# A graph attention layer on one core: the last stage in 25 units of 500 nodes, 20 of them between the closing steps of the edge loop

## The chip, the cores and the metric

The kernel runs on one core of a Trainium2 chip. The metric is the device time of one execution in microseconds (us). A core has a tensor engine (PE, with its weight loads shown apart as PEld), a vector engine (DVE), a scalar engine (ACT), GpSimd (POOL) and a queue engine (SP). SP and ACT issue ordinary DMAs, POOL issues DMAs with a list of row numbers (indirect ones), and all of them are carried by 16 DMA engines. Each engine works its instructions off in program order, so an instruction that waits holds up everything behind it on that engine.

## What is computed

The reference is a layer of graph attention over 12,500 nodes and 400,000 edges that are sorted by target node.

```python
h = relu(layernorm(x))
message = (h @ w_src + b_src)[src] + (h @ w_dst)[dst]
message = message * edge_weight * radial_mlp(edge_attr)      # 3 small layers
message = message @ w_sep + b_sep                            # 8 heads: 16 scores, 16 values each
score   = einsum(smooth_leaky_relu(message scores), alpha_dot)
att     = softmax of score over the edges of one target node
out     = x + segment_sum(value * att) @ w_proj + b_proj
```

The softmax's denominator is divided out last: each node has one row of 136 numbers, 128 sums of values and 8 sums of weights (one for each head), and the quotient goes through `w_proj` and is added to `x`.

## The kernel before, in words

A first stage works out the tables of `h @ w_src` and `h @ w_dst` and checks that the edges are sorted as the fast path needs. The number `bad` (L321) chooses between the fast path, `windows()`, and a slow one (L1450 to L1484). Only the fast one runs here.

`windows()` has 391 steps. A step takes 1,024 edges, which are two sections of 512 edges. A section's targets lie within a window of 64 nodes. In `step(k)` the instructions of several stages of different step numbers are written out one after the other: the gather of source rows on POOL (L862), the radial network, the message, the scores, and, 13 steps later (`LAG`), the sums of values and weights over each window. That last stage is step c = k - 13: `values` (L1060, L1062) multiplies the message by `w_v` and by the attention weight, `sums` (L1073, L1077) adds the edges up into a window of rows, `ob`, and SP stores it twice: whole into `win` (L1081) and, by two DMAs of 63 rows each to places that are read from a table, into `agg`, the table of node sums (L1085). A section's last node is often also the next one's first. Such nodes are put together apart from this: 13 blocks of 128 section ends are chained (L1117 to L1183), and the joined rows are scattered by POOL into `agg` after the windows (`scatter`, L1190 to L1197). The joined rows of the first eleven blocks are made during the main steps and kept in `obs_d`.

When the last main step is issued, the pool of loaded tiles is closed (`held.close()`), and 14 closing steps follow (j = 0 to 13, L1353 to L1363). They finish the 13 late steps and the last softmax group (its rows are moved by six small DMAs, `S<-Sp` at L980, and go through two scans, L1003 and L1008, an exponential and a transposition, L1030 and L1033). In each closing step from j = 2 on SP also loads the joined rows of one block (L1359), and POOL scatters them. Two buffers hold them. Blocks 11 and 12 are worked out in closing steps and behind them (L1340 to L1351 and L1366 to L1369).

All dependences between DMAs go by semaphores that the builder sets. Since the addresses of the `agg` stores are not known ahead, a store and a scatter wait for each other's landing, unless a line says that they need not. In the kernel before, that line is in `store` (L1086, only for sections from 768 on) and in `scatter`. Each DMA of SP and ACT counts up one of eight semaphores in turn, and is issued only when the previous DMA on the same semaphore has landed.

The last stage, `final` (L1386 to L1446), then loads `agg` by nine DMAs of 128 partitions with 12 rows each (L1396), and works on groups of 12 rows per partition: sums of weights plus 1e-16 (L1406), reciprocal (L1407), product (L1408), and for each four rows a transposition (L1419), a copy by ACT (L1422), the product with `w_proj` (L1430), the addition of `x` (L1433) and the store (L1434). `x` with its bias has been loaded by ACT's queue in closing steps j = 3 and later (L1382), as eight DMAs into one tile.

Of the kernel before, what the change touches and what calls it, by code (L numbers as in the profile page):

```python
# [21 lines left out]
F32 = mybir.dt.float32  # L22
BF16 = mybir.dt.bfloat16
I32 = mybir.dt.int32
# [8 lines left out]
H = 8  # L33
# [23 lines left out]
def gnn_kernel(ctx: ExitStack, tc: tile.TileContext, a: dict, out: bass.AP):  # L57
# [7 lines left out]
    NS = -(-E // SEC)  # L65
    NP = NS // 2
    NX = -(-NP // MP) * MP * PR
    assert NT * P == E and RC * RP == E and NT % TPI == 0 and NT % SORT_T == 0
    assert NB <= P and N < SKIP and E % T == 0 and NS % 34 == 0 and NP % 2 == 1

# [86 lines left out]
    with tc.tile_pool(name="node", bufs=2) as np_, tc.tile_pool(name="node1", bufs=1) as n1, \  # L157
# [19 lines left out]
        nc.vector.memset(cur[0:1, 0:1], -1)  # L177
        NH = NS // 17
        ends = n1.tile([NH, 17, 2], I32, name="ends")
        eb = n1.tile([P, NS, 2], I32, name="eb")  # L180
        wt = {name: const.tile(shape, F32, name="c_" + name) for name, shape in (
            ("b_src", [C, 1]), ("dot", [C, 1]), ("heads", [C, C]), ("fc_w1", [RAD, FC]), ("fc_b1", [FC, 1]),
# [4 lines left out]
        def load_targets():  # L187

            nc.sync.dma_start(out=cur[:, 1:CC + 1], in_=dst.rearrange("(p c) -> p c", p=P))
            at = dst[CC - 1:CC]  # L190
            with nc.allow_non_contiguous_dma(reason="single targets"):
                nc.sync.dma_start(out=cur[1:P, 0:1], in_=bass.AP(at.tensor, at.offset, [[CC, P - 1], [1, 1]]))
                at = dst[0:1]
                h = NH - 1
                nc.sync.dma_start(out=ends[0:h], in_=bass.AP(
                    at.tensor, at.offset, [[34 * SEC // 2, h], [SEC, 17], [SEC - 1, 2]]))
                at = dst[h * 17 * SEC:h * 17 * SEC + 1]
                nc.sync.dma_start(out=ends[h:NH, 0:16, :], in_=bass.AP(
                    at.tensor, at.offset, [[1, 1], [SEC, 16], [SEC - 1, 2]]))
                at = dst[(NS - 1) * SEC:(NS - 1) * SEC + 1]  # L200
                nc.sync.dma_start(out=ends[h:NH, 16, :], in_=bass.AP(
                    at.tensor, at.offset, [[1, 1], [E - 1 - (NS - 1) * SEC, 2]]))
# [103 lines left out]
        def fits():  # L306
# [11 lines left out]
            nc.tensor.matmul(tot[:, 0:1], cnt, ones[:, 0:1], start=False, stop=True, skip_group_check=True)  # L318
            sum_ = n1.tile([1, 1], F32, name="sum_")
            nc.vector.tensor_reduce(sum_, tot, AX.X, ALU.add)  # L320
            nc.vector.tensor_copy(bad, sum_)  # L321
            nc.sync.dma_start(out=ends_d[:, 1:2 * NS + 1].rearrange("o (p c) -> (o p) c", p=NH),
                              in_=ends.rearrange("p s i -> p (s i)"))
            none = n1.tile([1, 2], I32, name="none")
# [422 lines left out]
    def windows():  # L747
# [7 lines left out]
        with tc.tile_pool(name="ps", bufs=1, space=PSUM) as pp, \  # L755
# [327 lines left out]
            def store(c, f):  # L1083
                at = nc.sync.value_load(base[0:1, f, c:c + 1])
                st = nc.sync.dma_start(out=agg[ds(at, W - 1), :], in_=accs[c][f * W:(f + 1) * W - 1, :])  # L1085
                if 2 * c + 1 >= (NC - 1) * (P // 2):  # L1086
                    tc.declare_no_dep(st.ins, group="combined", reason="its rows follow those of the blocks")


            def load_x(i):  # L1090
# [99 lines left out]
            def scatter(g):  # L1190
# [4 lines left out]
                    bounds_check=N - 1, oob_is_err=False)  # L1195
                tc.declare_no_dep(st.ins, group="combined", reason="each node's row is written once")
                tc.add_to_no_dep_group("combined", st.ins)  # L1197

            comb = {}

            def combined(g):
                comb[g] = tail_pool.tile([P, ROW], F32, name="comb", bufs=2)
                return comb[g]

            stages = {0: lambda g: (block_load(g), block_rows(g)), 2: block_maxima, 4: block_factors,
                      5: block_columns, 6: block_totals, 8: block_out}
# [122 lines left out]
            held.close()  # L1329


            tail_pool = held.enter_context(tc.tile_pool(name="fin1", bufs=1, side="right"))
            x_fin = tail_pool.tile([P, NB, C], F32, name="x_fin")
            x_loads = load_xb(x_fin)
            last = NC - 1

            def out_rows(g):
                block_rows_out(g, combined(g))
                scatter(g)

            jobs = {
# [10 lines left out]
            assert SB * (NC - 1) + LAG + 1 == NP + 7  # L1352
            for k in range(NP, NP + LAG + 1):  # L1353
                step(k)
                j = k - NP
                if j in jobs:
                    jobs[j]()
                if 0 <= j - 2 < NC - 2:
                    nc.sync.dma_start(out=combined(j - 2), in_=obs_d[(j - 2) * P:(j - 1) * P, :])  # L1359
                    scatter(j - 2)  # L1360
                if j >= 3:
                    next(x_loads, None)
            for _ in x_loads:  # L1363
                pass
            block_rows(last)
            block_columns(last)  # L1366
            block_totals(last)
            out_rows(last)
            work.close()  # L1369
            with tc.tile_pool(name="fin", bufs=3) as fp:  # L1370
                final(fp, x_fin, lambda i: pp.tile([P, 4, P], F32, name=("pm0", "pm1", "V")[i % 3]),
                      lambda i: pp.tile([P, 4, C], F32, name=("p3", "pa", "m1")[i % 3]))


    XQ = 12
    out_v = out[0:NF * P, :].rearrange("(p t) c -> p t c", t=NF)
    agg_v = agg[0:NF * P, :].rearrange("(p t) c -> p t c", t=NF)

    def load_xb(x_fin):

        for t0, t1 in groups:
            nc.scalar.dma_start(out=x_fin[:, t0:t1, :], in_=xb_v[:, t0:t1, :])  # L1382
            yield
        nc.scalar.dma_start(out=x_fin[:tail, NF, :], in_=xb[NF * P:N, :])
        yield

    def final(fp, x_fin, turned, product):
        starts = list(range(0, NB, XQ))
        gs, qs, qTs = {}, {}, {}

        def load_g(i):

            gs[i] = fp.tile([P, XQ, ROW], F32, name="g", bufs=len(starts))
            for n, t0, t1 in blocks(starts[i], min(starts[i] + XQ, NB)):
                o = starts[i]
                nc.sync.dma_start(out=gs[i][:n, t0 - o:t1 - o, :],  # L1396
                                  in_=agg_v[:, t0:t1, :] if n == P else agg[NF * P:N, :].unsqueeze(1))

        def quotients(i):
            r = fp.tile([P, XQ, H], F32, name="r")  # L1400
            qs[i] = fp.tile([P, XQ, C], F32, name="q")
            g = gs.pop(i)
            for n, t0, t1 in blocks(starts[i], min(starts[i] + XQ, NB)):
                s = slice(t0 - starts[i], t1 - starts[i])
                m = t1 - t0
                nc.vector.tensor_scalar(r[:n, s, :], g[:n, s, C:ROW], 1e-16, None, op0=ALU.add)  # L1406
                nc.vector.reciprocal(r[:n, s, :], r[:n, s, :])  # L1407
                nc.vector.tensor_mul(  # L1408
                    qs[i][:n, s, :].rearrange("p t (h k) -> p (t h) k", h=H),
                    g[:n, s, 0:C].rearrange("p t (h k) -> p t h k", h=H),  # L1410
                    r[:n, s, :].unsqueeze(3).to_broadcast([n, m, H, C // H]))

        def turn(i):
            t0, t1 = quads[i]
            q, o = qs[t0 // XQ], t0 // XQ * XQ
            pt = turned(i)
            for t in range(t0, t1):
                n = rows(t)
                nc.tensor.transpose(pt[:, t - t0, :n], q[:n, t - o, :], ident[:n, :n])  # L1419
            w = (t1 - t0 - 1) * P + rows(t1 - 1)  # L1420
            qTs[i] = fp.tile([P, 4, P], F32, name="qT")
            nc.scalar.copy(qTs[i].rearrange("p u n -> p (u n)")[:, :w], pt.rearrange("p u n -> p (u n)")[:, :w])  # L1422

        def finish(i):
            t0, t1 = quads[i]
            qT = qTs.pop(i)
            py = product(i)
            for t in range(t0, t1):
                n = rows(t)
                nc.tensor.matmul(py[:n, t - t0, :], qT[:, t - t0, :n], w_proj, start=True, stop=True)  # L1430
            for n, u0, u1 in blocks(t0, t1):
                y = x_fin[:n, u0:u1, :]
                nc.vector.tensor_add(y, py[:n, u0 - t0:u1 - t0, :], y)  # L1433
                nc.sync.dma_start(out=out_v[:, u0:u1, :] if n == P else out[NF * P:N, :].unsqueeze(1), in_=y)  # L1434

        for i in range(len(starts)):
            load_g(i)
        quotients(0)
        turn(0)
        for i in range(Q):  # L1440
            if i % 3 == 1 and i // 3 + 1 < len(starts):
                quotients(i // 3 + 1)
            if i + 1 < Q:
                turn(i + 1)
            finish(i)


    unfit = nc.values_load(bad[0:1, 0:1], min_val=0, max_val=2 * E)
    with tc.If(unfit == 0) as fit:
        windows()  # L1450
    with fit.Else():
# [7 lines left out]
        with tc.tile_pool(name="bias", bufs=1) as op:  # L1459
# [15 lines left out]
        with tc.tile_pool(name="fin_b", bufs=3) as fp, tc.tile_pool(name="fin1_b", bufs=1) as f1, \  # L1475
                tc.tile_pool(name="fin_ps", bufs=2, space=PSUM) as fps, tc.manual_schedule():
            x_fin = f1.tile([P, NB, C], F32, name="x_fin")
            for _ in load_xb(x_fin):
                pass
            final(fp, x_fin, lambda i: fps.tile([P, 4, P], F32, name="pt"),  # L1480
                  lambda i: fps.tile([P, 4, C], F32, name="py"))


# [34 lines left out]
```

## Time and profile before

| | |
|---|---|
| median of three executions | 4234.25 us (4232.47 to 4238.16) |
| profiled execution | 4228.57 us, of which 4226.8 us are the span of the profile |
| busy in the span | PE 93%, DVE 74%, POOL 71%, ACT 45% |
| last main step's message leaves PE | about 4057 us |
| closing steps | about 4058 to 4144 us |
| last scatter issued, first load of `agg` issued | 4153.97, 4156.12 us |
| last addition | 4219.58 us |

How to read it: the profile gives for a line of the kernel the engine, the operation, the tile written and the tiles read, how often it ran, and what ended the idle time before it. The view by windows gives for a stretch of time how long each engine was busy, the granted clock of PE (1.00 is full), the mean busy share of the 16 DMA engines and the GB/s that they moved. The trace also holds each DMA packet with its size, start and duration. A packet is one contiguous run of bytes. The times in the views count from the start of the span.

### The profile page before, as it was taken

To read this page: it belongs to the slowest core of one execution; us is meant where nothing else is said; L and a number is where in the kernel's file an instruction comes from. 1 tells how busy PE (TensorE), PEld (TensorE's weight loads), DVE (VectorE), ACT (ScalarE), POOL (GpSimd) and SP (SyncE) were. 2 spreads that over 40 slices of the span, in tenths; PEclk is the share of its full clock that TensorE was granted. 3 is DMA by queue.
4 is the path that set the end of the run, shared out by engine and by line. 5 is a ranking of instruction groups with operands and counts; after the bars stand their busy time and mean duration, and the time that the engine had idled before them with its cause. 6 is when DMAs were issued, how large, how long until landed. Compare 5 with 4: busy or idle time off the path is not lost. (4 is left out here: it accounts for less than half of the span.)

```text
span 4226.8 us, 87991 instructions
## 1 busy us (share of the span) xinstructions
PE 3921.2 (93%) x29351; PEld 2394.1 (57%) x29351; DVE 3124.1 (74%) x6334; ACT 1919.2 (45%) x4597; POOL 2987.1 (71%) x3147
## 2 busy tenths in 40 slices
PE   6779999999999999999999999999999999999975
PEld 5345555555555555555555555555555555555554
DVE  6567777777777777777777777777777777777754
ACT  6344444444444444444444444444444444444421
POOL 0777777777777777777777777777777777777710
PEclk9889999999999999999999999999999999999988
DMA  6766776676776776676676676666766766666634
GB/s 217 218 193 178 189 195 178 195 194 185 189 198 188 187 194 187 182 195 189 186 193 194 183 192 179 179 184 185 187 183 180 189 180 183 188 178 185 184 86 160
DMA packets 593333, 783.08 MB, mean 185 GB/s; under 512 B 125553, under 2 KB 392302, under 8 KB 592740
## 3 DMA queue, kind: packets, MB, share of 16 engines
q1 hardware_dynamic: 384786, 514.16, 40.0%
q0 software_dynamic: 100416, 205.44, 22.2%
q10 hardware_dynamic: 107666, 57.76, 4.6%
q8 instruction: 234, 3.83, 0.4%
q14 instruction: 231, 1.89, 0.2%
HBM read 637.83 MB, written 139.30 MB: 184 GB/s over the span
## 5 line engine op out<-in xcount | busy, mean ns | idle before, releaser
L862 POOL DMA_INDIRECT gs<-t_src,idx x3125 | 2972.9, 951 | 1055.6 <-issue 802.6
L951 ACT ACTIVATE sl<-pa,c_b_a 128x512 f32<-128x512 f32 x782 | 536.9, 687 | 1021.1 <-PE pa L949 1006.6
L956 DVE SCALAR_TENSOR_TENSOR al<-pa,sl 128x512 f32<-128x512 f32 x782 | 540.4, 691 | 594.2 <-ACT sl L951 571.3
L1060 PEld LDWEIGHTS V<-c_w_v,mT 128*128 128x128 f32 x6048 | 746.6, 194 | 292.2 <-DVE ob L1077 122.3
L1060 PE MATMUL V<-c_w_v,mT 128*128 128x128 f32 x6048 | 879.1, 289 | 0.0
L949 PE MATMUL pa<-mT,c_w_a 128*128 128x512 f32 x1564 | 814.6, 603 | 3.5 <-DVE mT L943 2.6
L1062 DVE TENSOR_TENSOR pvx<-V,Pem 128x512 f32<-128x512 f32 x756 | 519.0, 687 | 243.7 <-PE V L1060 231.9
L929 PEld LDWEIGHTS pm<-ident,gs 128*128 128x128 f32 x3125 | 393.6, 142 | 421.3 <-issue 338.4
L1073 PEld LDWEIGHTS misc<-pvx,oh 128*64 128x64 f32 x6250 | 353.8, 138 | 408.4 <-ACT h L885 395.2
L921 DVE SCALAR_TENSOR_TENSOR rad<-p,c_fc_b,w_b 128x512 f32<-128x512 f32 x782 | 550.2, 745 | 39.5 <-PE p L913 4.3
L1073 PE MATMUL misc<-pvx,oh 128*64 128x136 f32 x6250 | 455.6, 288 | 116.1 <-ACT h L885 108.5
L943 DVE SCALAR_TENSOR_TENSOR mT<-pm,c_b_src,rad 128x512 f32<-128x512 f32 x782 | 550.7, 746 | 3.1 <-PE pm L936 3.1
L899 ACT ACTIVATE h<-p,b 128x512 f32<-128x512 f32 x391 | 287.5, 735 | 420.0 <-PE p L896 380.9
L929 PE MATMUL pm<-ident,gs 128*128 128x128 f32 x3125 | 472.3, 274 | 0.2 <-DMA gs<-t_src,idx 0.2
L913 PE MATMUL p<-h,w3b 64*128 64x512 f32 x1564 | 405.8, 596 | 12.5 <-ACT h L899 12.5
L936 PE MATMUL pm<-ohT,m 64*128 64x512 bf16 x2346 | 322.4, 381 | 0.0
L982 ACT ACTIVATE Sp<-m,b_s 128x512 f32<-128x512 f32 x192 | 131.9, 687 | 394.2 <-PE m L965 394.2
L881 PE MATMUL m<-eT,w1b 64*128 64x256 f32 x782 | 274.5, 431 | 27.6 <-DVE M L1003 18.1
L881 PE MATMUL misc<-eT,w1b 64*128 64x256 f32 x782 | 274.4, 431 | 0.0
L1046 DVE TENSOR_TENSOR oh<-lane,misc 128x504 f32<-128x504 f32 x391 | 262.2, 671 | 0.1
L896 PE MATMUL p<-h,w2b 64*64 64x256 f32 x3128 | 259.8, 402 | 0.6 <-DVE rad L921 0.6
L949 PEld LDWEIGHTS pa<-mT,c_w_a 128*128 128x128 f32 x1564 | 241.7, 195 | 20.7 <-DVE mT L943 6.2
(172 smaller groups left out, 3680.4 us busy)
## 6 DMA issues: line engine op xcount, KB each, us to landing
w_b<-in_edge_weight SPq DMA_DIRECT2D x390, 512.0 KB
d_b<-in_dst SPq DMA_DIRECT2D x390, 256.0 KB
gs<-t_src,idx POOLq DMA_INDIRECT x3125
e_t<-in_edge_attr ACTq DMA_DIRECT2D x390, 128.0 KB
sc_d<-Sp SPq DMA_DIRECT2D x192, 256.0 KB
win<-ob SPq DMA_DIRECT2D x391, 68.0 KB
agg<-ob SPq DMA_DIRECT2D x782, 33.5 KB
md<-t_dst SPq DMA_DIRECT2D x782, 32.0 KB
```

The source lines that it names most:

```text
L862: nc.gpsimd.indirect_dma_start(out=gs[:, t, :], out_offset=None, in_=t_src[:, :], in_offset=bass.IndirectOffsetOnAxis(ap=idx[:, t0 + t:t0 ...
L881: nc.tensor.matmul(p1[q], w1b[s, :], eTs[k][s, :], start=True, stop=True)
L913: nc.tensor.matmul(p3s[k][:, f, 0:SEC], w3b[s, :], h2s[k][s, :], start=True, stop=True)
L921: nc.vector.scalar_tensor_tensor(rad[:, s], p3[:, f, 0:n], b3, w_g[k][:, s], op0=ALU.add, op1=ALU.mult)
L929: nc.tensor.matmul(pms[k, f][:, t * T:(t + 1) * T], gs[:, t, :], ident, start=(t == 0), stop=False, is_transpose=True, skip_group_check=True)
L943: nc.vector.scalar_tensor_tensor(mTs[k][:, s], pms.pop((k, f))[:, 0:n], b_n, rad[:, s], op0=ALU.add, op1=ALU.mult)
L949: nc.tensor.matmul(pa[:, 0:n], w_a, mTs[k][:, f * SEC:f * SEC + n], start=True, stop=True)
L951: nc.scalar.activation(sl[:, 0:n], pa[:, 0:n], AF.Silu, bias=b_a, scale=1.0)
L956: nc.vector.scalar_tensor_tensor(al, pa, 0.25, sl, op0=ALU.mult, op1=ALU.add)
L1060: nc.tensor.matmul(V[:, t, :], mTs[c][:, o:o + T], w_v, start=True, stop=True)
L1062: nc.vector.tensor_mul(pvx[c][:, f, 0:n, 0:C].rearrange("p t (h k) -> p t h k", h=H), V[:, 0:n, :].rearrange("p t (h k) -> p t h k", h=H), ...
L1073: nc.tensor.matmul(acc[f * W:(f + 1) * W, :], ohs[c][:, f * TS + t, :], pvx[c][:, f, t, :], start=(t == 0), stop=(t == n - 1), skip_group_ ...
```

## The change

Nothing changes in the 391 main steps. Behind them:

- The last stage works in 25 units of 500 nodes, as 125 partitions with 4 rows each. A unit has one load of 125 x 2,176 bytes from `agg`, one of 125 x 2,048 bytes of `x`, and one store of 125 x 2,048 bytes.
- Units 0 to 19 are worked off within the closing steps: two per step for j = 4 to 11, one for j = 12 and 13, and two beside the last block. Units 20 to 24 follow the last scatter. Loads of early units and all loads of `x` are issued by ACT, loads of `agg` for the last five by SP.
- The first seven loads of `x` are issued ahead of closing step 0, the first seven loads of `agg` in closing step 3; later ones follow unit by unit.
- The joined rows of eleven blocks are loaded by one DMA (`ready`) ahead of closing step 0 and scattered by eleven instructions in a row.
- Stores of sections from 704 on do not wait for these eleven scatters. They are no longer exempt from waiting for the scatter of block 11.
- The check of the fast path also asks that section 704 begins at node 10,000 or later. In the given input it begins at node 10,146, so the fast path is taken.

```diff
             def store(c, f):
...
-                if 2 * c + 1 >= (NC - 1) * (P // 2):
-                    tc.declare_no_dep(st.ins, group="combined", reason="its rows follow those of the blocks")
+                if 2 * c >= EARLY_S:
+                    tc.declare_no_dep(st.ins, group="early", reason="its rows follow those of the early blocks")
+                    tc.add_to_no_dep_group("later", st.ins)
...
-            x_loads = load_xb(x_fin)
+            fin = held.enter_context(tc.tile_pool(name="fin", bufs=2, side="right"))
             last = NC - 1
+            ready = fin.tile([P, last - 1, ROW], F32, name="ready", bufs=1)
+            nc.sync.dma_start(out=ready, in_=obs_d[0:(last - 1) * P, :].rearrange("(g p) c -> p g c", p=P))
+            for g in range(last - 1):
+                comb[g] = ready[:, g, :]
+                scatter(g)
+            un = Units(fin, 8, 9, lambda u: pp.tile([P, 4, P], F32, name=("V", "pa")[u % 2]),
+                       lambda u: pp.tile([P, 4, C], F32, name=("p3", "m1")[u % 2]))
+            un.load_x(0, 7)
...
             for k in range(NP, NP + LAG + 1):
                 step(k)
                 j = k - NP
                 if j in jobs:
                     jobs[j]()
-                if 0 <= j - 2 < NC - 2:
-                    nc.sync.dma_start(out=combined(j - 2), in_=obs_d[(j - 2) * P:(j - 1) * P, :])
-                    scatter(j - 2)
-                if j >= 3:
-                    next(x_loads, None)
-            for _ in x_loads:
-                pass
+                if j == 3:
+                    for u in range(7):
+                        un.load_g(u)
+                    un.quotients(0)
+                    un.quotients(1)
+                    un.turn(0)
+                if j >= 4:
+                    un.run(2 if j < 12 else 1, EARLY)
             block_rows(last)
+            un.run(1, EARLY)
             block_columns(last)
+            un.run(1, EARLY)
             block_totals(last)
             out_rows(last)
...
-            with tc.tile_pool(name="fin", bufs=3) as fp:
...
+            un.open(EARLY, NU)
+            un.run(NU, NU)
+            un.close(NU)
...
+    UP, UT = 125, 4
...
+        def view(self, t, u):
+            return t[u * UN:(u + 1) * UN, :].rearrange("(p t) c -> p t c", t=UT)
...
+        def load_x(self, u0, u1):
+            for u in range(u0, u1):
+                if u < NU and u not in self.x:
+                    self.x[u] = self.pool.tile([UP, UT, C], F32, name="xu", bufs=self.nx)
+                    nc.scalar.dma_start(out=self.x[u], in_=self.view(xb, u))
...
+        def load_g(self, u):
+            self.g[u] = self.pool.tile([UP, UT, ROW], F32, name="g", bufs=self.ng)
+            eng = nc.scalar if u < EARLY else nc.sync
+            ld = eng.dma_start(out=self.g[u], in_=self.view(agg, u))
...
+        def finish(self, u):
+            qT, py, y = self.qT.pop(u), self.product(u), self.x.pop(u)
+            for t in range(UT):
+                nc.tensor.matmul(py[:UP, t, :], qT[:, t, :], w_proj, start=True, stop=True)
+            nc.vector.tensor_add(y, py[:UP], y)
+            nc.sync.dma_start(out=self.view(out, u), in_=y)
+            self.nf = u + 1
...
+        def run(self, n, end):
+            for _ in range(n):
+                u = self.nf
+                v = max(self.g, default=u) + 1
+                if v < end:
+                    self.load_g(v)
+                while self.nq < min(u + 3, end):
+                    self.quotients(self.nq)
+                while self.nt < min(u + 2, end):
+                    self.turn(self.nt)
+                self.finish(u)
+                self.load_x(u + 7, u + 8)
```

`quotients` is the addition, the reciprocal and the product of a unit on DVE (now written in place), `turn` four transpositions and ACT's copy, `finish` four products, the addition and the store.

More of the change, by code (lines that the diff above doesn't have):

```diff
@@ L67, in gnn_kernel @@
     NX = -(-NP // MP) * MP * PR
+    NU = 25
+    EARLY = 20
+    EARLY_S = (-(-2 * NS // P) - 2) * (P // 2)
     assert NT * P == E and RC * RP == E and NT % TPI == 0 and NT % SORT_T == 0
@@ L179, in gnn_kernel @@
         ends = n1.tile([NH, 17, 2], I32, name="ends")
+        lim = n1.tile([1, 1], I32, name="lim")
         eb = n1.tile([P, NS, 2], I32, name="eb")
@@ L192, in load_targets @@
                 nc.sync.dma_start(out=cur[1:P, 0:1], in_=bass.AP(at.tensor, at.offset, [[CC, P - 1], [1, 1]]))
+                at = dst[EARLY_S * SEC:EARLY_S * SEC + 1]
+                nc.sync.dma_start(out=lim, in_=at.unsqueeze(1))
                 at = dst[0:1]
@@ L320, in fits @@
             nc.vector.tensor_reduce(sum_, tot, AX.X, ALU.add)
-            nc.vector.tensor_copy(bad, sum_)
+            low = n1.tile([1, 1], F32, name="low")
+            nc.vector.tensor_scalar(low, lim, float(EARLY * (N // NU)), None, op0=ALU.is_lt)
+            nc.vector.tensor_add(bad, low, sum_)
             nc.sync.dma_start(out=ends_d[:, 1:2 * NS + 1].rearrange("o (p c) -> (o p) c", p=NH),
@@ L1197, in scatter @@
                 tc.add_to_no_dep_group("combined", st.ins)
+                if g < NC - 2:
+                    tc.declare_no_dep(st.ins, group="later", reason="its rows precede those of the later sections")
+                    tc.add_to_no_dep_group("early", st.ins)
+                else:
+                    tc.declare_no_dep(st.ins, group="early", reason="its rows follow those of the early units")
+                    tc.add_to_no_dep_group("later", st.ins)
             comb = {}
-            def combined(g):
-                comb[g] = tail_pool.tile([P, ROW], F32, name="comb", bufs=2)
-                return comb[g]
             stages = {0: lambda g: (block_load(g), block_rows(g)), 2: block_maxima, 4: block_factors,
@@ L1329, in windows @@
             held.close()
-            tail_pool = held.enter_context(tc.tile_pool(name="fin1", bufs=1, side="right"))
-            x_fin = tail_pool.tile([P, NB, C], F32, name="x_fin")
-            x_loads = load_xb(x_fin)
+            fin = held.enter_context(tc.tile_pool(name="fin", bufs=2, side="right"))
             last = NC - 1
+            ready = fin.tile([P, last - 1, ROW], F32, name="ready", bufs=1)
[6 more added lines that the diff above has]
+            un.load_x(0, 7)
             def out_rows(g):
-                block_rows_out(g, combined(g))
+                comb[g] = fin.tile([P, ROW], F32, name="comb")
+                block_rows_out(g, comb[g])
                 scatter(g)
@@ L1351, in windows @@
             }
-            assert SB * (NC - 1) + LAG + 1 == NP + 7
+            assert SB * (NC - 1) + LAG + 1 == NP + 7 and EARLY == 20
             for k in range(NP, NP + LAG + 1):
@@ L1365, in windows @@
+                if j >= 4:
+                    un.run(2 if j < 12 else 1, EARLY)
             block_rows(last)
+            un.run(1, EARLY)
             block_columns(last)
+            un.run(1, EARLY)
             block_totals(last)
             out_rows(last)
+            un.run(NU, EARLY)
+            un.close(EARLY)
             work.close()
-            with tc.tile_pool(name="fin", bufs=3) as fp:
-                final(fp, x_fin, lambda i: pp.tile([P, 4, P], F32, name=("pm0", "pm1", "V")[i % 3]),
-                      lambda i: pp.tile([P, 4, C], F32, name=("p3", "pa", "m1")[i % 3]))
@@ L1375, in gnn_kernel @@
[L1375 to L1445, printed above, removed]
@@ new lines, in windows, with __init__, quotients, turn @@
+            un.open(EARLY, NU)
+            un.run(NU, NU)
+            un.close(NU)
+    UP, UT = 125, 4
+    UN = UP * UT
+    assert N % UN == 0 and NU == N // UN
+    class Units:
+        def __init__(self, pool, nx, ng, turned, product):
+            self.pool, self.nx, self.ng, self.turned, self.product = pool, nx, ng, turned, product
+            self.x, self.g, self.qT = {}, {}, {}
+            self.nq = self.nt = self.nf = 0
+        def view(self, t, u):
[9 more added lines that the diff above has]
+            ld = eng.dma_start(out=self.g[u], in_=self.view(agg, u))
+            if u < EARLY:
+                tc.declare_no_dep(ld.ins, group="later", reason="their nodes follow those of the early units")
+                tc.add_to_no_dep_group("early", ld.ins)
+        def quotients(self, u):
+            g = self.g[u]
+            r = self.pool.tile([UP, UT, H], F32, name="r")
+            nc.vector.tensor_scalar(r, g[:, :, C:ROW], 1e-16, None, op0=ALU.add)
+            nc.vector.reciprocal(r, r)
+            q = g[:, :, 0:C].rearrange("p t (h k) -> p t h k", h=H)
+            nc.vector.tensor_mul(q, q, r.unsqueeze(3).to_broadcast([UP, UT, H, C // H]))
+            self.nq = u + 1
+        def turn(self, u):
+            g, pt = self.g.pop(u), self.turned(u)
+            for t in range(UT):
+                nc.tensor.transpose(pt[:, t, :UP], g[:, t, 0:C], ident[:UP, :UP])
+            self.qT[u] = self.pool.tile([P, UT, UP], F32, name="qT")
+            nc.scalar.copy(self.qT[u], pt[:, :, :UP])
+            self.nt = u + 1
+        def finish(self, u):
+            qT, py, y = self.qT.pop(u), self.product(u), self.x.pop(u)
+            for t in range(UT):
+                nc.tensor.matmul(py[:UP, t, :], qT[:, t, :], w_proj, start=True, stop=True)
+            nc.vector.tensor_add(y, py[:UP], y)
+            nc.sync.dma_start(out=self.view(out, u), in_=y)
+            self.nf = u + 1
+        def open(self, u0, u1):
+            for u in range(u0, u1):
+                self.load_g(u)
+            self.load_x(u0, u1)
+        def run(self, n, end):
+            for _ in range(n):
+                if self.nf >= end:
+                    return
+                u = self.nf
[8 more added lines that the diff above has]
+                self.load_x(u + 7, u + 8)
+        def close(self, end):
+            while self.nf < end:
+                self.run(1, end)
@@ L1474, in gnn_kernel @@
               ea_s.rearrange("(t p) c -> p t c", p=P), "b")
[L1475 to L1481, printed above, removed]
+        with tc.tile_pool(name="fin_b", bufs=3) as fp, tc.tile_pool(name="fin_ps", bufs=2, space=PSUM) as fps, \
+                tc.manual_schedule():
+            un = Units(fp, 10, 10, lambda u: fps.tile([P, 4, P], F32, name="pt"),
+                       lambda u: fps.tile([P, 4, C], F32, name="py"))
+            un.load_x(0, 7)
+            for u in range(7):
+                un.load_g(u)
+            un.run(NU, NU)
 def kernel(**inputs):
```

## Prediction

> **What bounds the kernel now.** I read the chain that ended last, then the waits and the timeline of the stretch behind the main steps, then the windows. The chain lies wholly in the last stage:
>
> ```profile
> DVE q L1408 0%; PE pm L1419 0%; PE m L1430 0%; PE p L1430 0%; DVE r L1407 0%; DVE x_fin L1433 0%; DVE r L1406 0%; DVEq L1406 0%
> ```
>
> Ahead of it stand the closing steps. The waits from 4040 to 4160 us, of SP's queue and of the engines, say what slows them:
>
> ```profile
> SPq L1085 <- DMA agg<-comb,ids: 20.6, 4, 11.4
> ...
> POOL agg L1192 <- DMA comb<-obs_d: 49.7, 10, 11.1
> ```
>
> Each store of windows waits for the scatter before it, each scatter for its load, and the load stands in SP's queue behind the store. So the closing steps last from 4058 to 4144 us, though PE is busy for only 5.5 of the 21 us from 4092 to 4113. Then the hand-over, in the timeline:
>
> ```profile
> 4153.97 0.90 POOL L1192 DMA_INDIRECT agg<-comb,ids  x1 [4.36 <-POOLq L1449]
> 4156.12 6.59 SPq L1396 DMA_DIRECT2D g<-agg  x10
> 4160.77 0.21 DVE L1406 TENSOR_SCALAR r<-g 128x96 f32<-128x96 f32 x1 [7.92 <-issue]
> 4161.02 0.75 DVE L1407 RECIPROCAL r<-r 128x96 f32<-128x96 f32 x1
> 4161.80 1.76 DVE L1408 TENSOR_TENSOR q<-g,r 128x1536 f32<-128x1536 f32 x1
> ```
>
> From the first load to the span's end are 4226.8 - 4156.1 = 70.7 us. They are what the change wants to hide.
>
> **What the DMAs can carry** decides this change, since every new load and store has 125 rows. Before has DMAs of 125 rows too: the clearing of `agg`, `agg<-z` (L139), packets of 2,720 bytes. The windows of its last burst and of the loads of `agg`:
>
> ```profile
> 228.00:240.00 12.00, 0.00 (x0) 0.00 (x0) 0.00 (x0) 0.00 (x0) 8.98 (x10) 0.51 0.45 155
> 4157.00:4171.00 14.00, 5.10 (x28) 4.70 (x29) 6.18 (x8) 1.76 (x3) 0.00 (x0) 0.64 1.00 403
> ```
>
> In the first row PE, DVE and ACT stand still and the DMA engines are busy for 0.45 only. In the second, loads of 128 rows fill all 16 (4158 to 4172: 420 GB/s, 26.2 per engine). The timeline shows the price of the first:
>
> ```profile
> 225.09 3.30 SPq L139 DMA_DIRECT2D agg<-z  x2
> ...
> 229.76 0.36 SPq L983 DMA_DIRECT2D sc_d<-Sp  x1
> ...
> 238.95 0.58 SPq L988 DMA_DIRECT2D S<-sc_d  x1
> ...
> 242.63 1.22 DVE L1003 TENSOR_TENSOR_SCAN M<-m,S 128x512 f32<-128x512 f32 x1 [17.79 <-DMA S<-sc_d]
> ```
>
> A 256 KB store behind two such DMAs took 8.8 us to land. The packet records say why. Of the 2,720-byte packets at most 7 or 8 are in flight at once, with two DMAs outstanding or four; of the 2,048-byte packets of 128 rows 17 to 21. The z bursts move 73 to 81 GB/s. If the 125 rows run on n engines, each of these carries 1/n of z and 1/16 of the rest. In the seven bursts n = 5 gives 21.7 to 27.9 GB/s per engine (first burst: 136 KB + 105 KB in 8.64 us), the saturated rate; n = 8 gives 22.0 in the first burst and less in the others. So I take five, always the same five, 25 packets on each: 5 x 26.2 = 131 GB/s.
>
> The Trainium skill, "DMA: Bandwidth & Descriptors", section "Why a DMA increments its semaphore by 16 and not by 1", says that a DMA issued by SP or ACT uses the largest number of engines up to 16 that divides its row count: five for 125. The trace agrees in a second case: the 63-row stores of windows end in nine small increments, those of 128 rows in sixteen. The same page's section "Anatomy of one DMA — SWDGE (gpsimd) path" fits 2.0 us plus bytes at 436 GB/s, under which nothing here would be bound by DMA; that is the first rival.
>
> **The change part by part.** A unit needs 125 x 2,176 bytes (272 KB, 2.08 us at 131 GB/s) and twice 256 KB (1.95 us each): 5.98 us of the five engines.
>
> *Its compute* costs less. DVE: addition 0.17 (between 0.16 for 8 columns and 0.20 for 96), reciprocal 0.35 (0.20 and 0.75), product 0.69 (0.29 for 128 columns, 1.76 for 1,536), addition of x 0.69: 1.90 us. PE: 0.60 + 1.06 = 1.66 us (L1419, L1430). A closing step without stalls takes PE 2.05 + 1.15 = 3.2 us (L1060, L1073), DVE 2.5 us. Two units in it: PE 6.5, DVE 6.3 us, and some 7.0 with their waits for each other. The DMAs of two units take 12 us. So from closing step 4 on, the five engines set the pace, not PE or DVE.
>
> *Ahead of closing step 0:* seven loads of x, 7 x 1.95 = 13.7 us of the five engines, from 4058.6 (the last main product on DVE, L943, whose tiles' room they take) to about 4075 with 2 us to land. Semaphores are taken in turn by eight DMAs, so a DMA waits for the landing of a stranger; before shows it as
>
> ```profile
> SPq L139 <- DMA e_t<-in_edge_attr: 7.7, 3, 3.7
> ```
>
> In the changed order the six `S<-Sp` (L980, at 4065 to 4069 before) come eight places behind the fifth to seventh load of x. They are then issued until 4078 or so, and the scan at 4070.46 (L1003), the exponential and the copy that ends at 4081.7 (L1033) move by 9 us (0 if no wait falls there, 13 if the loads also hold up ACT's work). ACT waits in its own queue as well: the seventh load for `ready`, and behind it stand the last `Silu` and the scores, some 6 us, within these 9.
>
> *The eleven scatters* need 11 x 1.25 us (the gather's 0.94 + 0.30), from about 4068 to 4082, and 2.2 us to land (4105.12 to the store at 4107.33). The first load of `agg`, now at 4081.7 + 9 = 4091, hides them. If each took the 6.75 us from the first scatter to the next store (4086.34 to 4093.09), they would end at 4144 and add 50 us; nothing but x loads in flight explains that one, so I leave it out.
>
> *What goes:* the waits of stores for scatters, 20.6 us, and eleven loads with their turns. That time is filled by the units. The new wait of a store for the scatter of block 11 holds only later stores, under 5 us, beside the same DMAs.
>
> *From 4091 on* the five engines carry 25 loads of agg, 18 of x and 25 stores: 52.0 + 35.1 + 48.8 = 135.9 us. ACT issues a load of x only when a unit's store has landed (eight buffers), but with five or so large DMAs outstanding the engines do not run dry. The windows' own stores cost each of the five 69.6 KB / 16 + 2 x 34.3 KB / 9 = 12 KB a step, 0.46 us, 13 times 6 us. First byte 1.0 us (4156.12 to the first packet of `agg` at 4157.11). The last block's chain (sums 4142.35 to load 4156.12 before, 13.8 us) runs beside the late stores and loads of x, which last about as long; I set 3 us for what is not covered. From the last data to the end 3 us (the last large packets end at 4222.2, the span at 4226.8, with two small stores between).
>
> **Sum:** 4091 + 1 + 135.9 + 6 + 3 + 3 = 4240 us of span against 4226.8: 13 us slower, 4242 against the profiled execution's 4228.57. That lies 5.7 us under the median shown, so on the median's scale 4234.25 + 13.2 = **4247.5 us**.
>
> Both ends: at the z bursts' 79 GB/s the 17.8 MB would take 225 us, 90 us more. But there the engines also carried the rest. At 131 with the delay ahead at nothing and the small stores hidden, it is 4240 - 9 - 6 = 4225.
>
> **The rivals.**
> *A, not slower: the rows spread over more engines.* With 16, a unit is 1.9 us of DMA and compute sets the pace. The loads land early, closing step 4 begins near 4090, eight steps of 7.0 us and two short ones end the last sums near 4153, the last loads go out 12 us later at 4165, and with 3.2 us to land, 12.5 for five units (five times 1.9 and the way in) and 6.7 to the end the span is 4187: -39 us, 4195. The change wins from six engines on, since 142 us then become 118. The 7 or 8 packets in flight (against 17 to 21 for sixteen, by ratio some 6 engines) leave this open; that 125 does not divide by 6, 7 or 8 speaks against it.
> *B, no change: five engines, but no delay ahead and full overlap:* 4225 of span, 4233.
> *C, slower still: the queues wait for one another.* A load of x waits for a store, the store in SP's queue for a window, ACT holds copies behind its load, and the five engines run dry for 1.5 us per early unit: 30 us more, 4277. The 8.8 us of the store at 229.76 speak for it.
> That the change does nothing is not possible here: section 704 begins above node 10,000.
>
> **How the numbers follow.** Forecast 0.55, A 0.15, B 0.15, C 0.15. Within 0.2% (8.5 us, about what a measurement of this kernel tells from no change) lie most of B and a little of the forecast: 0.18. Faster: A and a little of B, 0.18. Slower: 0.64. The range reaches from below B, 4222, over the forecast to most of C, 4285; A is left out.
>
> **What would show it.** Right: after 4091 the DMA share stays near 0.3 to 0.4 with 130 to 170 GB/s while PE and DVE wait on loads of g or x; L1003 of the last group near 4079; at most 8 packets of 2,048 or 2,176 bytes in flight; closing steps of 10 us and more. Wrong: loads of units at 300 GB/s, PE over 90% in the closing steps, the last scatter before 4170.

## The result, and the profile after

The changed kernel takes 4273.41 us (median of four runs, 4271.84 to 4279.97), the kernel before beside it 4233.36 us (four runs, 4232.17 to 4238.16): a ratio of 1.0095, 95% interval 1.0081 to 1.0108. It is slower by 40 us. The forecast was 4247.5 us, 13 us slower, within 4222 to 4285.

The profiled execution took 4274.37 us, its span 4272.6 us. The profile page of the changed kernel, the chain that ended last:

```profile
DMA g<-agg 0%; DMA agg<-comb,ids 0%; PE p L1446 0%; PE m L1446 0%; PE pa L1438 0%; PE V L1438 0%; DVE g L1432 0%; DVE xu L1447 0%; DVE r L1430 0%; SPq L1421 0%; DVE r L1429 0%; POOLq L1476 0%
```

It now begins with transfers: the load of a unit's sums, and ahead of it the last scatter. Before, it held only DVE and PE. The windows of the closing steps, the hand-over and the last units (us, then busy time and instructions of PE, PEld, DVE, ACT and POOL, granted clock, DMA share, GB/s):

```profile
4113.00:4144.00 31.00, 17.01 (x140) 15.29 (x138) 16.94 (x41) 3.56 (x9) 0.00 (x0) 0.82 0.36 134
4144.00:4171.00 27.00, 16.35 (x99) 14.85 (x100) 9.52 (x23) 2.75 (x10) 0.00 (x0) 0.69 0.36 131
4171.00:4210.00 39.00, 26.48 (x196) 24.03 (x195) 21.74 (x50) 5.53 (x15) 0.97 (x1) 0.85 0.35 129
...
4230.00:4250.00 20.00, 3.16 (x13) 2.40 (x13) 1.32 (x5) 0.56 (x2) 0.90 (x1) 0.50 0.22 72
4250.00:4273.00 23.00, 10.40 (x60) 9.65 (x60) 9.31 (x20) 2.88 (x5) 0.00 (x0) 0.65 0.30 104
```

In none of them is PE or DVE busy for 70% of the time, and in none do the 16 DMA engines reach a share of 0.4. That is the sign the prediction named: five engines full, eleven nearly empty. The packet records say it outright. From the first load of `agg` at 4101.46 us to the end, at most 8 packets of 2,048 or 2,176 bytes are in flight; while any is, the mean is 4.9; and for only 11.3 of the 171.1 us none is. Each DMA of a unit also ends in small increments, packets of 4 bytes: five behind each of the five late loads of `agg` (the first at 4249.09 to 4249.48 us). In the experiments below there are 14 behind a late store of 126 rows, 16 behind one of 128 and one behind one of 127. So the number five does not hang on packets in flight alone.

What waits is in SP's queue (total us, times, longest):

```profile
SPq L1093 <- DMA agg<-ob: 55.4, 18, 6.5
...
SPq L1093 <- DMA xu<-xb: 11.8, 5, 5.7
...
SPq L1093 <- DMA agg<-comb,ids: 5.7, 1, 5.7
```

The waits of stores for scatters went from 20.6 to 5.7 us, as predicted. The stores of windows now wait for their own forerunners: 55.4 us from 4062 us on, against 12.2 in the closing steps of the kernel before (4040 to 4160 us). With units of 128 rows (e1 below) it is 16.0, so it is the narrow transfers that hold these stores up.

The timeline at the start of the closing steps (start, duration, engine, line, operation, tiles):

```profile
4062.90 12.23 ACTq L1416 DMA_DIRECT2D xu<-xb  x7
...
4075.17 0.34 ACT L1048 COPY pvx<-Pem 128x32 f32<-128x32 f32 x2 [12.47 <-DMA win<-ob]
...
4084.17 4.90 SPq L988 DMA_DIRECT2D S<-Sp  x6
...
4090.65 1.22 DVE L1011 TENSOR_TENSOR_SCAN M<-m,S 128x512 f32<-128x512 f32 x1 [5.24 <-DMA S<-Sp]
```

ACT stands in its queue for 12.2 us until the seventh load of `x` is issued. The last scores come behind it and end at 4080.4, their six small transfers start at 4084, behind stores of windows in SP's queue, and the scan at 4090.65 (before: 4070.46; the prediction named 4079). The closing steps with two units take 11.5 to 15.4 us each, as it said. And the hand-over to the last five units:

```profile
4229.99 0.84 SPq L1140 DMA_DIRECT2D rr<-win  x2
...
4236.72 0.28 PE L1172 MATMUL misc<-ident,rr 28*128 28x28 f32 x1 [10.71 <-DMA rr<-win]
...
4241.47 0.90 POOL L1201 DMA_INDIRECT agg<-comb,ids  x1 [36.03 <-POOLq L1476]
4245.17 2.71 SPq L1421 DMA_DIRECT2D g<-agg  x5
4250.02 0.18 DVE L1429 TENSOR_SCALAR r<-g 125x32 f32<-125x32 f32 x1 [9.63 <-DMA g<-agg]
```

**One yardstick for all runs.** The main steps, the same in all kernels here, end at different times from run to run: the last message on DVE (`mT<-pm`) starts at 4058.2 us in the profile of before and at 4064.0 in that of after, and in the experiments with untouched main steps between 4057.8 and 4064.4. So I also compare the *tail*, from that instruction to the span's end: 168.6 us before, 208.6 after. The difference, 40.0 us, is that of the medians: all of the loss lies in the tail.

### The profile page after: what moved, and what is told of

The parts are those of the page before. It is cut to its first block, busy times and chain, and to the rows that moved or that the text cites. A ratio compares the mean times of both kernels' runs of the same rounds, so it can differ in the third digit from the quotient of the medians.

```text
span 4272.6 us, 88068 instructions
## 1 busy us (share of the span) xinstructions
PE 3937.2 (92%) x29357; PEld 2404.3 (56%) x29357; DVE 3129.8 (73%) x6379; ACT 1919.5 (45%) x4597; POOL 2987.3 (70%) x3147
## 5 line engine op out<-in xcount | busy, mean ns | idle before, releaser
L921 PE MATMUL p<-h,w3b 64*128 64x512 f32 x1564 | 406.6, 597 | 13.8 <-ACT h L907 13.7
```

Source lines behind the costliest of these rows:

```text
L921: nc.tensor.matmul(p3s[k][:, f, 0:SEC], w3b[s, :], h2s[k][s, :], start=True, stop=True)
```

## The experiments

The first four ran on one chip against a kernel before of 4229.41 us. "Theory W" is that the 125-row transfers keep to five engines and set the pace; its main rival "Q" is that the queues wait for one another.

**e1_rows128: the units on 128 partitions.**

```diff
-    EARLY = 20
+    EARLY = 19
...
-    UP, UT = 125, 4
+    UP, UT = 128, 4
...
-            return t[u * UN:(u + 1) * UN, :].rearrange("(p t) c -> p t c", t=UT)
+            o = min(u * UN, N - UN)
+            return t[o:o + UN, :].rearrange("(p t) c -> p t c", t=UT)
```

Expected: 

> The changed kernel with units of 512 nodes on 128 partitions in place of 500 on 125; unit 24 begins at node 11,988 and writes 300 rows a second time, and 19 units are early in place of 20. Theory W (width): the 125-row transfers are carried by five of the sixteen DMA engines (at most 8 of their packets in flight in the changed kernel, 17.8 MB at 111 GB/s, the five without work for only 11 of the last 171 us), so they set the pace of the closing steps. Then 128 rows run on all sixteen, a unit's transfers take some 2 us in place of 6 to 7, and the time falls to 4195 to 4215 us, with 17 or more packets in flight and the seven loads of x done in 5 to 6 us in place of 18. Rival Q (queues): the five engines are busy only because transfers wait for one another in ACT's and SP's queues (the wait of ACT for landed stores, 65.6 us in all); then the order is the same and the time stays above 4255 us.

Measured: 4197.24 us, ratio 0.9925 (0.9909 to 0.9942). The tail is 136.6 us, 72 us shorter than with 125 rows. A store of a late unit takes 0.82 us with 17 to 18 packets in flight. The closing steps in the windows of this kernel:

```profile
4097.00:4163.00 66.00, 54.56 (x494) 49.79 (x492) 52.86 (x126) 13.79 (x38) 0.97 (x1) 0.97 0.63 207
```

PE is busy for 83% and DVE for 80% of the 66 us, with a clock of 0.97: compute is the bound again. Order, queues and buffers are the same but for one early unit less, so Q is out. It also comes near the price of rival A of the prediction: 32 us less than the kernel before, where A had 39.

**e2_split: the 125 rows kept, each transfer cut in two.**

```diff
...
+        parts = (slice(0, 112), slice(112, UP))
...
-            nc.sync.dma_start(out=self.view(out, u), in_=y)
+            for p in self.parts:
+                nc.sync.dma_start(out=self.view(out, u)[p], in_=y[p])
```

(and so for the loads of `x` and `agg`). Expected: 

> The changed kernel with the same 125-row units, each transfer issued as two: partitions 0 to 111 and 112 to 124. Units, bytes, buffers and order are as they were; there are 75 more DMAs. Theory W: 112 rows spread over sixteen engines and 13 over thirteen, so the time falls nearly as far as with 128 rows, 4195 to 4225 us. Rival Q: more DMAs in the same queues and in the rotation of eight semaphores make it no better or worse than 4273, 4265 to 4300 us.

Measured: 4207.23 us, ratio 0.9943 (0.9926 to 0.9960), a tail of 142.7 us. Units, bytes and buffers are those of the change, and the spread alone wins 66 us. With 75 DMAs more, and every second one of only 13 rows, the tail is 6 us longer than e1's. The Trainium skill, "DMA: Bandwidth & Descriptors", section "Rules for kernel authors", advises against two transfers to disjoint partition halves, since both spread over all 16 engines anyway; here the measurement decides otherwise, because the whole does not spread and its parts do.

**e3_xlater: the first loads of x moved from ahead of closing step 0 to closing step 2.**

```diff
-            un.load_x(0, 7)
...
+                if j == 2:
+                    un.load_x(0, 7)
```

Expected: 

> The changed kernel with 125 rows; only the first seven loads of x are issued in closing step 2, behind the last exponential, and not ahead of closing step 0. Both theories: the rows of scores (the six small S<-Sp transfers) go 14 us earlier, the first scan is near 4076 in place of 4090.65 us. Theory W: the time of the five engines is still needed, only 18 us of it come later and before the first load of agg, so of the 14 us only some 5 remain: 4262 to 4270 us. Rival L (the delay ahead of closing step 0 is a loss of its own, on the path): the whole 14 us are won, 4255 to 4261 us.

Measured: 4268.14 us, ratio 1.0088 (1.0071 to 1.0105). The scan comes 12.6 us behind the last message in place of 26.6 (before: 12.3), so the loads were the whole of that delay. But the tail falls only by 2.5 us, to 206.1, and the median by 5.3, at the small end of what W expected: the 18 us of transfers now stand between the scan and the first unit. Rival L is out.

**e4_joined: the joined rows' part alone, with the last stage of the kernel before** (the edit is against that kernel).

```diff
+            x_fin = fin.tile([P, NB, C], F32, name="x_fin", bufs=1)
+            ready = x_fin[:, NB - 12:NB, :].rearrange("p t c -> p (t c)")[:, 0:(last - 1) * ROW]
...
+            for g in range(last - 1):
+                comb[g] = ready[:, g, :]
+                scatter(g)
...
-                if 0 <= j - 2 < NC - 2:
-                    nc.sync.dma_start(out=combined(j - 2), in_=obs_d[(j - 2) * P:(j - 1) * P, :])
-                    scatter(j - 2)
```

Expected: 

> The joined rows' part of the change alone: one load of eleven blocks and eleven scatters in a row, with the new exemptions from waiting; the last stage, its loads of x and its units are those of the kernel before (the rows lie in the part of the x tile that is loaded last). Theory S: the waits of stores for scatters (20.6 us in SP's queue, with 49.7 us of POOL for its loads) were on the path of the closing steps, and without them the last sums come 15 to 25 us earlier: 4208 to 4222 us. Rival: loads of x and the last blocks' chain take their place and the time stays within 5 us of before, 4228 to 4238 us.

Measured: 4215.71 us, ratio 0.9965 (0.9951 to 0.9979); the tail is 156.1 us, 12.5 less than before. SP's waits in this kernel from 4040 to 4160 us:

```profile
SPq L1093 <- DMA agg<-ob: 22.1, 20, 4.5
...
SPq L1093 <- DMA agg<-comb,ids: 2.9, 1, 2.9
```

This half of the change is a gain, and of the 20.6 us of waiting some 13 to 15 were on the path. Beside this kernel, which has that half of the change, the changed one is 58 us slower (52.5 us of tail): that is what the units lost.

**The rule on row counts.** The next four (before: 4233.42 us beside them) ask what decides the number of engines. "Theory D": the largest divisor of the row count up to 16.

**e5_rows126**, one row more than the change: `UP, UT = 126, 4`, with the view of e1 and 20 early units. Expected: 

> Units of 504 nodes on 126 partitions, 20 of the 25 early as in the changed kernel; the last one begins at node 11,996 and writes 100 rows a second time. One row per DMA more than in the changed kernel. Theory D (the number of engines is the largest divisor of the row count up to 16): 126 rows run on 14 engines, some 22 GB/s each and 310 GB/s in all, so a unit's transfers take 2.5 us and compute sets the pace as with 128 rows: 4193 to 4207 us, 14 to 17 packets in flight. Rival M (sixteen only for multiples of 16, few engines for any other count; or the change came from unit size and alignment): 4255 us and more. The Trainium skill, DMA: Bandwidth & Descriptors, section Why a DMA increments its semaphore by 16 and not by 1, states the rule of theory D.

Measured: 4205.55 us, ratio 0.9939 (0.9922 to 0.9955), at most 18 packets in flight. One row more per DMA takes 68 us off.

**e6_rows127**, two rows more: `UP, UT = 127, 4`, 19 early units. Expected: 

> Units of 508 nodes on 127 partitions, 19 early; the last one begins at node 11,992 and writes 200 rows a second time. Theory D: 127 has no divisor but 1 up to 16, so one engine carries every unit at the 22 to 26 GB/s that an engine had in the changed kernel and in the loads of the kernel before. 25 units of 797 KB are 19.9 MB, 760 to 910 us of transfers from some 4062 us on: 4830 to 4990 us, with one or two packets in flight. Rival M (a count that does not divide well is spread as 125 is, five to eight engines): 4230 to 4290 us.

Measured: 4882.12 us, ratio 1.1543 (1.1524 to 1.1562). The windows of this kernel:

```profile
4200.00:4800.00 600.00, 96.54 (x531) 85.07 (x531) 58.90 (x138) 17.18 (x47) 1.87 (x2) 0.55 0.07 28
```

A DMA share of 0.07 is one engine of sixteen (0.06) and little else; while a packet of the units is in flight there are on average 1.0 of them, at 25 GB/s. Rival M, an uneven spread of odd counts, is out: 125, 126, 127 and 128 rows gave 4273, 4206, 4882 and 4197 us. The Trainium skill, "DMA: Bandwidth & Descriptors", section "Why a DMA increments its semaphore by 16 and not by 1", states the rule of theory D, with 127 partitions on one engine as an example; the increments (5, 14, 1 and 16) and the times agree with it at each of these counts.

**e7_early: 128 rows, the first loads of agg ahead of closing step 3, those of x behind it.**

```diff
...
+                j = k - NP
+                if j == 3:
+                    for u in range(7):
+                        un.load_g(u)
                 step(k)
...
                 if j == 3:
-                    for u in range(7):
-                        un.load_g(u)
+                    un.load_x(0, 7)
```

Expected: 

> Units of 128 rows with two loads moved: the first seven loads of agg are issued ahead of closing step 3 and not behind it (the eleventh scatter is issued at 4078.5 us with 128 rows, the loads at 4086.9), and the first seven of x follow in closing step 3 and no longer stand ahead of closing step 0. With transfers on sixteen engines compute and the chain of the last softmax group are what is left. Theory P: the scores' rows leave SP at 4066 in place of 4070 us and units 0 and 1 fill part of the 12 us from 4085 to 4097 in which PE is busy for 6.3: 4186 to 4193 us against 4197 for 128 rows alone. Rival: the closing steps are bound by DVE and PE from 4097 on and what is done earlier only waits elsewhere, 4194 to 4199 us.

Measured: 4197.81 us, ratio 0.9916 (0.9900 to 0.9933). In the trace the tail is 131.5 us, 5 less than e1's, but in that run the main steps ended 6.6 us later, and the times do not tell the two apart: 4197.81 us lies where the rival had it. Whether the move is worth something is left undecided.

**e8_z100: the kernel before, its clearing of agg in DMAs of 100 rows.**

```diff
-    zc = 5
...
-    z = const.tile([RP, zc * ROW], F32, name="z")
+    zc, ZP = 5, 100
...
+    z = const.tile([ZP, zc * ROW], F32, name="z")
...
```

There are 25 of these DMAs in place of 20, each a fifth smaller, with the same packets.

Expected: 

> The kernel before, with only the clearing of agg changed: 25 DMAs of 100 rows in place of 20 of 125 rows, the same 2,720-byte packets. It tells whether the row count alone sets the spread, away from the last stage. Theory D: 100 rows run on ten engines, the bursts move 130 to 160 GB/s in place of 73 to 81 with 12 or more packets in flight, a 256 KB store behind two of them lands in some 5 us in place of 8.8, and the wait of the first scan (17.8 us) gets shorter by 3 to 12 us: ratio to before 0.997 to 1.000. Rival M: 7 or 8 packets in flight as with 125 rows and no change of the waits; five DMAs more then cost 0 to 5 us.

Measured: 4215.73 us, ratio 0.9961 (0.9948 to 0.9973), a larger gain than either side expected. The bursts move 90 to 169 GB/s with 10 to 13 packets in flight (before: 73 to 81 GB/s, 7 or 8), and the longest wait for a store of scores (`sc_d<-Sp`), 8.8 us before, is 5.1 us. The timeline of this kernel:

```profile
221.25 1.21 DVE L1003 TENSOR_TENSOR_SCAN M<-m,S 128x512 f32<-128x512 f32 x1
```

The bracket is gone that in the kernel before said 17.79 us of waiting at 242.63. The scan runs 21 us earlier, and by the ratio some 17 of them reach the end.

**Together.** c1_both has e1 and e8, c2_both_early e7 and e8, c3_z96 e1 and a clearing in DMAs of 96 rows (`zc, ZP = 5, 96`). Expected of c1: 

> Units of 128 rows (which alone gave 4197 us) together with the clearing in 25 DMAs of 100 rows (which alone gave a ratio of 0.9961 to the kernel before, by taking the wait of the first scan away). The two lie 3,800 us apart and share nothing but the rule on row counts. If both are losses of their own they add up: 0.9925 x 0.9961 = 0.9886, some 4179 to 4186 us. Rival: the head start is taken back in the main steps by the gather, whose issues are POOL's 2,973 us, and less than half of the 17 us remains: 4188 to 4197 us.

Of c2: 

> As the one with units of 128 rows and the clearing by 100, and with the first loads of agg ahead of closing step 3 and those of x behind it. Alone this move gave no difference to be seen (4197.8 against 4197.2). If it is worth nothing, the time is within 6 us of the kernel without it; if the 4 us by which the first scan comes earlier are real, 3 to 6 us less.

Of c3: 

> Units of 128 rows and the clearing in 26 DMAs of 96 rows with one of 20 rows for the rest: sixteen engines in place of ten for each. Theory D: 16 packets in flight and 150 to 250 GB/s in the bursts; since with 100 rows the wait of the first scan was already gone, nothing or at most 5 us are left to win: 4174 to 4186 us.

These three ran on another chip, on which the kernel before took 5325.01 us, with steps of 13 us in place of 10. Why is open: in the trace of c1 PE stands idle in the main steps without a releaser that the profile shows ("issue"), and POOL waits for PE. The ratios were 0.9957 (0.9940 to 0.9974), 0.9955 (0.9935 to 0.9976) and 0.9947 (0.9923 to 0.9971). They do not tell the three apart, and the sum, 0.9886, is not there: 20 to 28 us were won, and on the other chips the two gains make some 48. The tails are 140 to 146 us, near e1's 136.6, which speaks for the units' part holding on that chip as well; the clearing's is not to be seen, since the last message starts anywhere from 5140 to 5163 us in the three traces. So c3 ran once more, as d1_z96_again. Expected: 

> The same kernel as c3 (units of 128 rows, clearing in 26 DMAs of 96 rows and one of 20), once more, since the chip of the three runs before took 5325 us for the kernel before, 1,090 us more than the others did, in main steps of 13 us in place of 10. There its gain was 0.5%, or 27 us. On a chip on which the kernel before takes 4229 to 4233 us: if the gains of the two parts add up, a ratio of 0.985 to 0.990, 4170 to 4190 us; if the main steps take the head start back, 0.990 to 0.993, 4190 to 4203 us.

Measured, on a chip on which the kernel before takes 4230.26 us: **4182.99 us, ratio 0.9891 (0.9874 to 0.9907)**. The product of the two ratios is 0.9925 x 0.9961 = 0.9886 (e8 with 100 rows, this run with 96): on this chip the gains add up. The last message starts at 4040.7 us, 17.5 earlier than in the kernel before, more than the 6.6 by which that start varies among the other runs, and the tail, 137.3 us, is e1's. This version beats both kernels, the changed one by some 90 us on the medians of two comparisons.

## Why the prediction was right and wrong

- **Five engines set the pace: right, shown.** e1, e2 and e5 change little but the spread (e2 not even the size of the units) and win 66 to 76 us; e6 narrows it and loses 609 against the changed kernel.
- **The sum: its term "135.9 us of DMA" was mis-sized, and that is the step that failed.** From the first load of `agg` on, 5,375 packets of 2,048 bytes with a mean of 90 ns and 3,125 of 2,176 bytes with 93 ns make 777 us, on five engines 155.4: 19.5 us more than forecast. The rate, 26.2 GB/s per engine, came from the loads of `agg` in the kernel before, whose packets have 6,528 bytes (248 ns each, median). A nearer row stood in the same profile: the stores of `out`, 2,048 bytes in 86 ns. But the smaller packets explain no more than half of the miss: with their medians, 84 and 88 ns, the term would be 145.3. The other 10 us lie in few packets: 223 of the 8,500 took over 120 ns, and what held them up stays open. At the end of e6, where stores run alone on one engine, a packet of 2,048 bytes starts every 80 ns, which is 25.6 GB/s; by an estimate from that pace the bytes need 139 us, so packet size may have cost as little as 3.
- **The delay ahead of the units, forecast 9 us: 14.3 us, and its main cause was the part I had set second.** ACT stood for 12.2 us in its queue (forecast 6, within the 9), and the scores behind it end 16.4 us after the last message in place of 7.7. The rest of the delay passes in SP's queue, ahead of the six small transfers. From the last message to the first load of `agg` it is 37.5 us, forecast 32.8: 4.7 of the missing us. e3 shows that this delay, though real, was worth only 2.5 us of tail: the engines need the time of those loads wherever they stand.
- **The rest, 13 us for windows, first byte, hand-over and end: 15.7.** The hand-over alone took 25.6 us, from the start of the last sums on PE at 4219.54 to the load at 4245.17 (before 13.8), but in 20 of these packets of the units were in flight. 19.5 + 4.7 + 2.7 = 26.9 us is, but for 0.1, what lies between the forecast's 13.2 and the 40.0 measured.
- **Scatters hidden, store waits under 5 us: right but for a little** (last of eleven issued at 4088.91, ahead of the first load of `agg`; 5.7 us). What I did not price is what this part won by itself, 12.5 us of tail in e4; in the changed kernel the units lost more than that.
- **The rivals.** A's condition failed (the units' packets moved at 111 GB/s while any was in flight), but its price (39 us won) was nearly met by e1 (32). B fell with the rate. C's number (4277) was the nearest and its mechanism is wrong: the five engines ran dry for 3.0 us between 4101 and 4221 us, not for 30. That the range held the result is in part luck: it reached that far for C's sake, and the mechanism I forecast had been priced at a third of the loss.

## What to carry to other kernels

Look at the row count of every DMA before its bytes: 125 rows ran on five engines and 127 on one, while 126 and 128 rows ran wide, and the sign in a trace is a low DMA share beside waits for transfers, with few packets in flight. When a rate is carried from one row to another, take it from packets of the same size, and leave room for packets that are held up: here they cost as much again. And where transfers set the pace, moving one does not win the wait that it causes; widening it does.

## What the runs showed of the hardware that was not expected

- On average an engine has about one packet in flight: while the units' transfers ran the mean was 1.0 on one engine (e6, from 4200 to 4800 us, at most 2) and 4.9 on five (at most 8). A packet took 84 ns for 2,048 bytes, 88 for 2,176, 248 for 6,528 and 272 for 7,168 (medians): 24.4, 24.7, 26.3 and 26.4 GB/s.
- DMAs of few engines hold up wide ones: in the kernel before, the 256 KB store behind two 125-row DMAs took 8.8 us to land, and with 100 rows in the clearing (e8) the longest such wait was 5.1 us; that run as a whole was some 17 us shorter, of 4230.
- One chip ran the kernel before in 5325 us, 26% above the others, at a granted clock of 0.93 against 0.98. In the traces that exist from that chip (c1, c2 and c3) the busy times of DVE, ACT and POOL are those of the other chips. What lengthened its main steps stays open.
